# Ten buffers instead of six for the rows of x, with 4096 contiguous bytes per partition in each load and store

## The chip, the cores and the metric

The kernel runs on one NeuronCore of a Trainium2 chip. The metric is the device time of one execution in microseconds (us). The kernel before took 1952.6 us, the median of three runs (1951.16 to 1956.97 us).

## What is computed

One layer of a relational graph network with a layer norm ahead of it: 12,500 nodes of 256 floats, 212,500 edges sorted by their destination, 8 types of edges.

```
h = jnp.maximum(_layernorm(x, axis=-1), 0.0)
hx = jnp.einsum('ni,rio->rno', h, weight)            # 8 relations
agg = jax.ops.segment_sum(hx[edge_type, src], dst, num_segments=12500)
out = x + agg * 0.5**0.5 + h_bias + (h @ loop_weight) * 0.5**0.5
```

The kernel turns the sums around: for each destination and type it first adds up the rows h[src], and multiplies the eight sums of a destination by the eight weights afterwards.

## The kernel before

**Tiles and gathers.** The edges are cut into 1581 tiles of 128, two tiles to a unit. For each tile the row h[src] of each edge is fetched from DRAM into a tile msg of 128 rows by 1 KB. For most tiles that is one indirect DMA, issued by GpSimd (POOL, L936, `gather`); I number them from 0 in the order of issue. For 50 tiles far into the program the sync and scalar queues fetch single rows instead (L965). A matmul of each msg tile with a one-hot matrix (TensorE, L1031, `edge_sums`) sums rows by destination and type in PSUM, and VectorE adds the sum of each unit to a ring of accumulators (L1064, `add_sums`). Each group of 128 destinations that is complete is multiplied by the weights (L1238) and stored.

**What a gather waits for.** 33 buffers hold two msg tiles each. The first 100 gathers of the program read raw rows of x, since h isn't there yet; these take one of eight completion counters (DMASW0 to DMASW7) in turn, so that each waits until the gather eight before it has landed. Gather 100 is the first that reads h; it waits until all of h has been stored. In `goal` (L948 to L952) the order of the program lets the gathers run ahead of the sums by a count of tiles that rises by 4 for each unit; `gather` adds a wait on the last matmul of the unit before (L945, "no faster than the sums"). So gather 72, the first of its step, waits for the end of tile 25, and gather 80 for the end of tile 29. From gather 66 on a gather also needs a msg buffer that has been read.

**The normalised rows.** x is cut into 26 pieces: 24 of 512 rows (four rows of 1 KB for each of 128 partitions), one of 128 and one of 84 rows (L805 to L809). A piece goes through five steps. The sync queue (SP) loads it into a buffer xt (`load_rows`, L886). VectorE takes the statistics of each 128 rows (L828, `moments`). For each bunch of pieces ScalarE takes a root (L864) and VectorE the reciprocal (L868, in `close`). ScalarE normalises in place (L872). SP stores the piece to the DRAM tensor h32 (L895, in `rest`). ScalarE and VectorE treat the msg tiles that were gathered from x in the same way, by the same lines.

**The order around them.** The order of each engine's instructions is written out by hand (`manual_schedule`), and each engine works through its own list. Pieces 0 to 3 come first. Then the loop over the tiles t (L1441) normalises one piece in each of three steps out of four and a batch of four msg tiles in the fourth, which I call a period: 3 pieces and 4 tiles. The loop's step 28 normalises the last piece, after which `load_weights` (L1363) loads the bias, w and wl through SP, and ScalarE scales w six steps later (L1378). Since VectorE works in order, the add of unit u (L1064) stands behind the statistics of the pieces of its step: unit 9's add stands behind the statistics of piece 20, unit 11's behind those of piece 23. The matmuls of a unit need a free PSUM bank of four; the wait for it is put on the last matmul of the unit before, so the end of tile 25 waits for the add of unit 9, and the end of tile 29 for that of unit 11.

**The buffers of the pieces.** xt comes from a pool of ROWS = 6 buffers (L334). `norm_rows(i)` (L888) first issues the load of piece i + 4 into the buffer of piece i - 2, which waits until the store of piece i - 2 has ended; the store of piece i is issued later, when ScalarE has normalised it. SP works in order too: while a load waits, the stores behind it aren't issued. A DMA of SP also takes one of eight completion counters (DMAHW0 to DMAHW7) in turn, so no more than eight are on their way.

Of the kernel before, what the change touches and what calls it, by code (L numbers as in the profile page):

```python
# [9 lines left out]
F32 = mybir.dt.float32  # L10
# [13 lines left out]
P = 128  # L24
# [4 lines left out]
XG = 4  # L29
# [56 lines left out]
SHARED = 3  # L86

ROWS = 6
FIRST = 4


# [157 lines left out]
def kernel(  # L249
# [12 lines left out]
    N, D = x.shape  # L262
# [30 lines left out]
    w = const.tile([P, KC, R * D], F32, name="w")  # L293
# [34 lines left out]
    with ExitStack() as main:  # L328
# [4 lines left out]
        ep = main.enter_context(tc.tile_pool(name="ep", bufs=1))  # L333
        rowp = main.enter_context(tc.tile_pool(name="rowp", bufs=ROWS))  # L334
        idx = main.enter_context(tc.tile_pool(name="idx", bufs=2))
# [469 lines left out]
        for d in range(0, N, XG * P):  # L805
            k = min(XG, (N - d) // P)
# [3 lines left out]

        def rows_of(a, i):
            d, k, n = pieces[i]
            return a[d : d + k * n].rearrange("(k p) d -> p k d", p=n)

        bunch = []

        def moments(rows_, n, then, begun=None):

            if not bunch:
                bunch.append(small.tile([P, 2 * BATCH, 6], F32, name="stats") if begun is None else begun)  # L820
                if n < P:
                    nc.vector.memset(bunch[0], 0.0)
            stats = bunch[0]
            here = rows_ if begun is None else rows_[:-SHARED]
            for row in rows_:
                k = sum(len(r) for r, _, _ in bunch[1:])
                if begun is None or len(bunch) - 1 < len(here):
                    in_run("stats", nc.vector.bn_stats(stats[:n, k, :], row), row is here[-1])  # L828
                bunch.append(([row], n, None))
            bunch.append(([], n, then))  # L830
# [49 lines left out]
        xts = {}  # L880

        def load_rows(i):
            if i < len(pieces):
                _, k, n = pieces[i]
                xts[i] = rowp.tile([P, XG, D], F32, tag="rows", name="xt")
                nc.sync.dma_start(xts[i][:n, :k, :], rows_of(x, i))  # L886

        def norm_rows(i):  # L888
            d, k, n = pieces[i]
            xt = xts.pop(i)  # L890
            if i > 1:
                load_rows(i + ROWS - 2)

            def rest():
                nc.sync.dma_start(rows_of(h32, i), xt[:n, :k, :])  # L895

            moments([xt[:n, j, :] for j in range(k)], n, rest)

# [103 lines left out]
        def load_offsets(u0):  # L1002
            n = min(REGS, NU - u0)
            b, q = row_of(u0)
            _, vals = nc.values_load_multi_w_load_instructions(
                place[b][0:1, q : q + n], engines=[DVE], min_val=0, max_val=RING - 1,
                skip_runtime_bounds_check_because="clamped to the ring where it is computed")
            for i, v in enumerate(vals):
                offsets[u0 + i] = v
# [279 lines left out]
        with tc.manual_schedule():  # L1289

            load = prepare(0)
            load[0]()
            for i in range(ROWS):
                load_rows(i)
            make_identity(nc, ident)
            iota_i = marks.tile([P, XG * GROUP], I32, tag="mark0", name="iota_i")
# [29 lines left out]
            for i in range(2):  # L1326
                norm_rows(i)
# [19 lines left out]
            after.pop(0)()  # L1347
            for i in range(2, FIRST):
                norm_rows(i)
# [83 lines left out]
            load_offsets(0)  # L1433
            done["norm"] = FIRST
            for t in range(0, 2 * BATCH, BATCH):
# [5 lines left out]
            for t in range(NT):  # L1441
# [12 lines left out]
                if t % BATCH == BATCH - 1:  # L1454
                    if done["norm"] < len(pieces):
                        after = batch(t + 1 + BATCH)
                    elif done["scaled"] <= t + 1 + 2 * BATCH:
                        after = batch(done["scaled"], 2 * BATCH)
                        after.append(lambda t=done["scaled"]: begin_batch(t))
                elif done["norm"] < len(pieces):  # L1460
                    for i in range(1 if NT > 400 else 20):
                        if done["norm"] < len(pieces):
                            norm_rows(done["norm"])
                            done["norm"] += 1
                            if t % BATCH % 2 or NT <= 400 or done["norm"] == len(pieces):
                                after += close()
                    if NT <= 400:
                        for f in after:
                            f()
                        after = []  # L1470
                    if done["norm"] == len(pieces):
                        for f in after:
                            f()
                        after = []
                        norms_end(t)
# [91 lines left out]
```

## Time and profile before

| what | value |
|---|---|
| median of three runs | 1952.6 us |
| the profiled execution | 1951.46 us |
| its span, first to last instruction | 1949.8 us |
| TensorE busy (PE) | 1702.0 us, 87% |
| GpSimd busy (POOL) | 1455.6 us, 75% |
| VectorE busy (DVE) | 1305.0 us, 67% |
| ScalarE busy (ACT) | 157.2 us, 8% |
| mean granted TensorE clock | 0.953 |
| DMA, mean rate | 143 GB/s |
| busy share of the 16 DMA engines, 60 to 120 us | 0.98 |
| the same, 400 to 1900 us | 0.46 |

The times of the trace count from the span's start; the profiled execution took 1.7 us beyond its span. The shares are means over parts that differ: ScalarE is busy for two thirds of the first 200 us and hardly at all behind them, and the DMA engines are full in the first 120 us only, in which the pieces are loaded and stored. "Releaser" in a row is what ended the idle time ahead of an instruction; "issue" means that the profile shows none.

### The profile page before, as it was taken

What the parts mean: (1) busy time and instruction counts of PE and PEld (TensorE: products, weight loads), DVE (VectorE), ACT (ScalarE), POOL (GpSimd) and SP (SyncE); (2) the same over time, 40 slices, a digit from 0 to 9 for tenths busy, and PEclk for the clock granted to TensorE, in tenths of its full rate; (3) what the DMA queues carried; (4) which work ended last, traced back from release to release, by engine and by line L of the source; (5) the groups of instructions that cost most, each with busy time, mean ns of one, the idle gap of its engine ahead of it and who ended that gap; (6) DMA issues with size and microseconds to landing.
All of it is one profiled execution on the core that took longest, in us unless ns stands there. A gap on an engine that the chain in (4) does not pass through costs nothing.

```text
span 1949.8 us, 40539 instructions
## 1 busy us (share of the span) xinstructions
PE 1702.0 (87%) x10161; PEld 1460.0 (75%) x10161; DVE 1305.0 (67%) x3284; ACT 157.2 (8%) x333; POOL 1455.6 (75%) x1557
## 2 busy tenths in 40 slices
PE   2358999999998999889898899998889889899998
PEld 2247898998887777777777777777777777687887
DVE  7668766787765687656677665578566567665652
ACT  6778200000000000000000000000000000000000
POOL 7767777777777777777777777777777777777774
PEclk9559999999999999999999999999999999999999
DMA  9984454544444444444544444444444444444442
GB/s 291 329 281 129 125 152 123 153 133 141 122 142 131 132 143 114 138 131 121 152 132 121 141 128 124 142 121 142 131 120 140 130 125 132 121 141 126 131 121 82
DMA packets 158423, 279.41 MB, mean 143 GB/s; under 512 B 35441, under 2 KB 109191, under 8 KB 158183
## 3 DMA queue, kind: packets, MB, share of 16 engines
q0 software_dynamic: 73488, 200.77, 35.6%
q1 hardware_dynamic: 76648, 72.73, 12.1%
q10 hardware_dynamic: 8046, 3.30, 0.9%
q8 instruction: 80, 1.31, 0.3%
q14 instruction: 161, 1.31, 0.2%
HBM read 251.06 MB, written 25.60 MB: 142 GB/s over the span
## 4 chain that ended last, share of the span: by engine, by line
PE 40%; DMA 23%; POOL 20%; issue 8%; DVE 6%; ACT 3%; SPq 0%; DVEq 0%; POOLq 0%; ACTq 0%; PEldq 0%
PE po L1238 20%; DMA msg<-h,gidx 20%; POOL msg L936 20%; PE ps L1031 18%; ACT msg L872 1%; DVE acc L1064 1%; DMA h<-xt 1%; DVE stats L828 1%; DMA xt<-in_x_dram 1%; DVE acc L1106 1%; PE pt L1088 1%; ACT xt L872 1%; DMA msg<-h 1%; DVE oh L993 1%; PE pt L1137 1%
## 5 line engine op out<-in xcount | busy, mean ns | idle before, releaser
L936 POOL DMA_INDIRECT msg<-h,gidx x1431 | 1358.7, 949 | 437.4 <-issue 363.8
L1031 PEld LDWEIGHTS ps<-oh,msg 128*128 128x128 f32 x6324 | 929.1, 197 | 390.5 <-DMA msg<-h,gidx 248.4
L1031 PE MATMUL ps<-oh,msg 128*128 128x136 f32 (+1 forms) x6324 | 1010.5, 289 | 204.5 <-DMA msg<-h,gidx 120.8
L1238 PE MATMUL po<-w,acc 128*128 128x256 f32 (+1 forms) x3136 | 890.3, 389 | 7.8 <-DVE acc L1064 7.2
L1064 DVE TENSOR_TENSOR acc<-acc,ps 128x352 f32 x791 | 408.6, 517 | 391.2 <-PE ps L1031 381.9
L1238 PEld LDWEIGHTS po<-w,acc 128*128 128x128 f32 (+1 forms) x3136 | 519.4, 193 | 45.5 <-DVE acc L1064 10.4
L1106 DVE SCALAR_TENSOR_TENSOR acc<-types,pt 128x256 f32<-128x256 bf16 x688 | 248.6, 412 | 68.6 <-PE pt L1088 64.4
L993 DVE TENSOR_TENSOR oh<-fixed,cols 128x544 f32<-128x544 f32 x396 | 282.8, 714 | 0.0
L936 POOL DMA_INDIRECT msg<-in_x_dram,gidx x100 | 94.9, 949 | 39.2 <-issue 34.2
L1238 PE MATMUL po<-wl,self_t 128*128 128x256 f32 (+1 forms) x392 | 114.6, 418 | 6.8 <-DVE acc L1064 4.5
L1238 PEld LDWEIGHTS po<-wl,self_t 128*128 128x128 f32 (+1 forms) x392 | 72.9, 208 | 15.5 <-DVE acc L1064 5.6
L1226 DVE TENSOR_TENSOR xr<-xr,po 128x256 f32<-128x256 f32 (+1 forms) x98 | 40.5, 413 | 24.0 <-PE po L1238 17.3
L872 ACT ACTIVATE msg<-msg,shift,rstd 128x256 f32<-128x256 f32 x100 | 50.8, 587 | 6.3 <-DVE stats L836 4.6
L872 ACT ACTIVATE xt<-xt,shift,rstd 128x256 f32<-128x256 f32 x98 | 50.0, 587 | 13.1 <-DVE shift L869 13.1
L1253 DVE TENSOR_TENSOR xr<-xr,po 128x256 f32<-128x256 f32 (+1 forms) x98 | 41.2, 421 | 10.6 <-PE po L1238 7.3
L828 DVE BATCH_NORM_STATS2 stats<-xt 128x6 f32<-128x256 f32 x98 | 34.1, 411 | 14.9 <-DMA xt<-in_x_dram 14.6
L1088 PE MATMUL pt<-ident,hr 128*128 128x128 f32 (+1 forms) x196 | 39.0, 282 | 4.6 <-DMA hr<-h 2.7
L1093 DVE COPY self_t<-pt 128x256 f32<-128x256 f32 (+1 forms) x98 | 40.5, 414 | 3.1 <-PE pt L1088 2.9
L1160 DVE CAST types<-pt 128x512 bf16<-128x512 f32 x22 | 15.2, 691 | 40.5 <-PE pt L1156 40.5
L455 DVE TENSOR_SCALAR moves<-fixed 128x271 int32<-128x271 int32 (+1 forms) x90 | 40.5, 450 | 1.6 <-DVE acc L1064 0.5
L457 DVE COPY_PREDICATED fixed<-moves,fixed 128x311 int32<-128x311 int32 (+14 forms) x90 | 38.0, 422 | 3.1
L1088 PEld LDWEIGHTS pt<-ident,hr 128*128 128x128 f32 (+1 forms) x196 | 25.7, 152 | 7.1 <-DMA hr<-h 2.9
(166 smaller groups left out, 348.8 us busy)
## 6 DMA issues: line engine op xcount, KB each, us to landing
msg<-h ACTq DMA_DIRECT2D x3200, 1.0 KB
msg<-h SPq DMA_DIRECT2D x3200, 1.0 KB
msg<-h,gidx POOLq DMA_INDIRECT x1431, 4.7
xt<-in_x_dram SPq DMA_DIRECT2D x24, 512.0 KB
h<-xt SPq DMA_DIRECT2D x24, 512.0 KB
xr<-in_x_dram SPq DMA_DIRECT2D x23, 512.0 KB
hr<-h SPq DMA_DIRECT2D x23, 512.0 KB
out_dram<-xr SPq DMA_DIRECT2D x22, 512.0 KB
```

The costliest lines, as they stand in the source:

```text
L455: nc.vector.tensor_single_scalar(m, packed[:, :n], 1 << (bit + k), op=ALU.bitwise_and)
L828: in_run("stats", nc.vector.bn_stats(stats[:n, k, :], row), row is here[-1])
L872: nc.scalar.activation(row, row, AF.Relu, bias=shift[:n, j : j + 1], scale=rstd[:n, j : j + 1])
L936: i = nc.gpsimd.indirect_dma_start(out=msg[t], out_offset=None, in_=table[:, :], in_offset=bass.IndirectOffsetOnAxis(ap=gidx[b][:, at : at ...
L993: j = nc.vector.tensor_tensor(o[:, k : k + v, :i, :width], iota_f[:, :width].unsqueeze(1).unsqueeze(1).to_broadcast([P, v, i, width]), of. ...
L1031: j = nc.tensor.matmul(ps[:, c, first : first + width], m[:, c * P : (c + 1) * P], o[:, :width], start=(i == 0 and c == 0), stop=(end and ...
L1064: i = nc.vector.tensor_tensor(a, a, ps, op=ALU.add)
L1088: in_run("turns", nc.tensor.transpose(pst[:, c, :n], rows_[:n, c * P : (c + 1) * P], ident[:n, :n]), c == KC - 1)
L1093: nc.vector.tensor_copy(got["self", g][:, :, :n], pst[:, :, :n])
L1106: i = nc.vector.scalar_tensor_tensor(acc[:, :, r, s0 : s0 + n], of, float(r + 1), pst[:, :, :n], op0=ALU.is_equal, op1=ALU.mult)
L1238: i = nc.tensor.matmul(got["out", g][:n], lhs, rhs, start=(r == R and c == 0), stop=(r == R - 1 and c == KC - 1))
L1253: nc.vector.tensor_add(rows_[:n, k, :], rows_[:n, k, :], got["out", g][:n])
```

## The change

The number of buffers of the pieces goes from 6 to 10. The pool keeps its 6; pieces whose number modulo 10 is 6 to 9 go into four parts of the tile of the weights, w (128 x 2 x 2048 floats), which is filled with the weights only after the last piece. The load of piece i + 8 (was i + 4) is now issued behind the store of piece i, no longer ahead of the statistics of piece i; it still waits for the store of piece i - 2. Ten loads (was six) are issued at the start. And a piece's rows are dealt out differently: partition p holds the four rows 4p to 4p + 3 of the piece, which lie together in DRAM (4096 bytes), where it held the rows p, 128 + p, 256 + p and 384 + p (four stretches of 1024 bytes). Loads and stores both do so. The loads and stores of the groups at L1179 to L1184 and L1255 to L1259 stay as they were.

```diff
@@ -86,6 +86,7 @@
 SHARED = 3
 
 ROWS = 6
+STAGED = 10
 FIRST = 4
 
 
@@ -810,7 +811,7 @@
 
         def rows_of(a, i):
             d, k, n = pieces[i]
-            return a[d : d + k * n].rearrange("(k p) d -> p k d", p=n)
+            return a[d : d + k * n].rearrange("(p k) d -> p k d", p=n)
 
         bunch = []
 
@@ -882,17 +883,20 @@
         def load_rows(i):
             if i < len(pieces):
                 _, k, n = pieces[i]
-                xts[i] = rowp.tile([P, XG, D], F32, tag="rows", name="xt")
+                j = i % STAGED - ROWS
+                if j < 0:
+                    xts[i] = rowp.tile([P, XG, D], F32, tag="rows", name="xt")
+                else:
+                    xts[i] = w.rearrange("p c (a k d) -> p (c a) k d", k=XG, d=D)[:, j, :, :]
                 nc.sync.dma_start(xts[i][:n, :k, :], rows_of(x, i))
 
         def norm_rows(i):
             d, k, n = pieces[i]
             xt = xts.pop(i)
-            if i > 1:
-                load_rows(i + ROWS - 2)
-
             def rest():
                 nc.sync.dma_start(rows_of(h32, i), xt[:n, :k, :])
+                if i > 1:
+                    load_rows(i + STAGED - 2)
 
             moments([xt[:n, j, :] for j in range(k)], n, rest)
 
@@ -1290,7 +1294,7 @@
 
             load = prepare(0)
             load[0]()
-            for i in range(ROWS):
+            for i in range(STAGED):
                 load_rows(i)
             make_identity(nc, ident)
             iota_i = marks.tile([P, XG * GROUP], I32, tag="mark0", name="iota_i")
```

PE, POOL, DVE and ACT keep the order of their instructions; only names of tiles change (w in the place of xt). SP's order changes. At the start of the program SP issued, before, the last two of its six loads, then the stores of pieces 0 and 1, the loads of pieces 6 and 7 and the store of piece 2:

```order
L886 DMA xt_152<-in_x_dram 128x4x256
L886 DMA xt_154<-in_x_dram 128x4x256 [waits DMAHW0_49]
L895 DMA h32_57<-xt_144 128x4x256 [waits DMAHW3_49,DMAHW1_49,Activation_49]
L895 DMA h32_57<-xt_146 128x4x256 [waits DMAHW4_49,DMAHW2_49,Activation_49]
L886 DMA xt_291<-in_x_dram 128x4x256 [waits DMAHW1_49]
L886 DMA xt_298<-in_x_dram 128x4x256 [waits DMAHW2_49]
L895 DMA h32_57<-xt_148 128x4x256 [waits DMAHW5_49,Activation_49]
```

The same place now, from piece 4's load on (one stretch of 1024 elements for each partition, w_64 for pieces 6 to 9):

```order
L891 DMA xt_152<-in_x_dram 128x1024
L891 DMA xt_154<-in_x_dram 128x1024 [waits DMAHW0_49]
L891 DMA w_64<-in_x_dram 128x1024 [waits DMAHW1_49]
L891 DMA w_64<-in_x_dram 128x1024 [waits DMAHW2_49]
L891 DMA w_64<-in_x_dram 128x1024 [waits DMAHW3_49]
L891 DMA w_64<-in_x_dram 128x1024 [waits DMAHW4_49]
L897 DMA h32_57<-xt_144 128x1024 [waits DMAHW5_49,Activation_49]
L897 DMA h32_57<-xt_146 128x1024 [waits DMAHW6_49,Activation_49]
L897 DMA h32_57<-xt_148 128x1024 [waits DMAHW7_49,Activation_49]
L891 DMA xt_354<-in_x_dram 128x1024 [waits DMAHW5_49,DMAHW0_49]
```

Four more loads stand ahead of the first store, and the next load (piece 10) stands behind the store of piece 2. In the middle of the pieces, SP before ran from the store of piece 10 (xt_529) to the load of piece 20 (xt_842):

```order
L895 DMA h32_57<-xt_529 128x4x256 [waits DMAHW0_49,Activation_49]
L895 DMA h32_57<-xt_573 128x4x256 [waits DMAHW1_49,Activation_49]
L886 DMA xt_709<-in_x_dram 128x4x256 [waits DMAHW0_49]
L895 DMA h32_57<-xt_583 128x4x256 [waits Activation_49]
L886 DMA xt_753<-in_x_dram 128x4x256 [waits DMAHW4_49,DMAHW1_49]
L886 DMA xt_762<-in_x_dram 128x4x256 [waits DMAHW3_49]
L895 DMA h32_57<-xt_619 128x4x256 [waits DMAHW6_49,Activation_49]
L895 DMA h32_57<-xt_663 128x4x256 [waits DMAHW7_49,Activation_49]
L886 DMA xt_798<-in_x_dram 128x4x256 [waits DMAHW6_49]
L895 DMA h32_57<-xt_673 128x4x256 [waits Activation_49]
L886 DMA xt_842<-in_x_dram 128x4x256 [waits DMAHW7_49,DMAHW2_49]
```

Now, from the store of piece 10 (xt_354) to the load of piece 20 (xt_751):

```order
L897 DMA h32_57<-xt_354 128x1024 [waits Activation_49]
L891 DMA w_64<-in_x_dram 128x1024 [waits DMAHW6_49,DMAHW3_49]
L897 DMA h32_57<-xt_357 128x1024 [waits Activation_49]
L891 DMA w_64<-in_x_dram 128x1024 [waits DMAHW5_49,DMAHW0_49]
L897 DMA h32_57<-xt_528 128x1024 [waits Activation_49]
L891 DMA xt_751<-in_x_dram 128x1024 [waits DMAHW7_49,DMAHW2_49]
```

The load of piece 20 stood behind the store of piece 15 and stands behind that of piece 12 now; a store and a load alternate.

## The prediction

> **What bounds the kernel now.** I began with the page: the busiest engine is TensorE with 87% of the span, then POOL with 75%. A share doesn't say who waits for whom, so the next view is the waits, for the long middle (500 to 1900 us).
>
> ```profile
> span 1949.8 us, 40539 instructions
> PE 1702.0 (87%) x10161; PEld 1460.0 (75%) x10161; DVE 1305.0 (67%) x3284; ACT 157.2 (8%) x333; POOL 1455.6 (75%) x1557
> ```
>
> ```profile
> POOL msg L936 <- issue: 288.4, 945, 0.3
> PE ps L1031 <- DMA msg<-h,gidx: 117.9, 212, 2.6
> ```
>
> The last number of a row is the longest wait. POOL never waits longer than 0.3 us there, and TensorE waits 117.9 us for gathered rows: the gathers set the pace. The page's groups count the gathers (x1431 and x100), and the timeline of POOL shows them one by one: start, duration, and in brackets the idle time before.
>
> ```profile
> L936 POOL DMA_INDIRECT msg<-h,gidx x1431 | 1358.7, 949 | 437.4 <-issue 363.8
> ...
> L936 POOL DMA_INDIRECT msg<-in_x_dram,gidx x100 | 94.9, 949 | 39.2 <-issue 34.2
> ```
>
> ```profile
> 4.86 1.11 POOL L936 DMA_INDIRECT msg<-in_x_dram,gidx  x1 [2.23 <-DVE bound_o L1320]
> 92.76 0.94 POOL L936 DMA_INDIRECT msg<-in_x_dram,gidx  x1 [0.30 <-ACT msg L872]
> 94.01 0.95 POOL L936 DMA_INDIRECT msg<-in_x_dram,gidx  x1 [0.30 <-issue]
> ...
> 100.54 0.94 POOL L936 DMA_INDIRECT msg<-in_x_dram,gidx  x1 [5.59 <-issue]
> ...
> 112.07 0.94 POOL L936 DMA_INDIRECT msg<-in_x_dram,gidx  x1 [1.83 <-issue]
> ...
> 137.06 0.95 POOL L936 DMA_INDIRECT msg<-h,gidx  x1 [0.30 <-ACT wl L1379]
> ...
> 205.66 0.95 POOL L936 DMA_INDIRECT msg<-h,gidx  x1 [1.01 <-ACT msg L872]
> ...
> 1931.94 0.95 POOL L936 DMA_INDIRECT msg<-h,gidx  x1 [0.30 <-issue]
> ```
>
> Two gathers follow each other in 94.01 - 92.76 = 1.25 us: 0.95 busy and 0.30 idle. There are 1531 (1431 + 100), and 1530 steps of 1.25 are 1912.5 us of the 1927.1 between the first and the last. Only three gathers idle longer: gather 72 at 100.54, gather 80 at 112.07 and gather 154 at 205.66. Beyond the usual 0.30 they cost 5.29 + 1.53 + 0.71 = **7.53 us**; the rest is gathers that took a little over 0.95. So whatever happens to the pieces of x, the kernel can win 7.53 us at most, and what makes POOL wait longer is lost one for one.
>
> Why those waits? Timelines of DVE, PE and SP near 100 us:
>
> ```profile
> 96.37 1.40 DVE L828 BATCH_NORM_STATS2 stats<-xt 128x6 f32<-128x256 f32 x4 [2.89 <-DMA xt<-in_x_dram]
> 98.44 0.52 DVE L1064 TENSOR_TENSOR acc<-acc,ps 128x352 f32 x1
> 99.02 2.09 PE L1031 MATMUL ps<-oh,msg 128*128 128x104 f32 x8 [5.72 <-DVE acc L1064]
> 109.97 0.52 DVE L1064 TENSOR_TENSOR acc<-acc,ps 128x352 f32 x1
> 110.55 2.09 PE L1031 MATMUL ps<-oh,msg 128*128 128x104 f32 x8 [2.13 <-DVE acc L1064]
> ```
>
> The statistics of piece 20 wait for its load; the add of unit 9 (98.44) stands behind them; the end of tile 25 (99.02) waits for the add, and gather 72 for tile 25. Gather 80 hangs in the same way on unit 11's add at 109.97. The waits of DVE and SP between 30 and 125 us:
>
> ```profile
> DVE stats L828 <- DMA xt<-in_x_dram: 14.6, 6, 3.1
> SPq L886 <- DMA h<-xt: 54.0, 16, 6.4
> ```
>
> Late pieces hold DVE up six times, 14.6 us; SP stands 54.0 us ahead of a load until an old piece is stored, which is the missing buffer.
>
> **The change, part by part.** *Earlier loads.* The load of piece 20 was issued with 21's at 87.67, behind the store of piece 15. Now it stands behind the store of piece 12, whose normalising began at 64.35:
>
> ```profile
> 64.35 2.07 ACT L872 ACTIVATE xt<-xt,shift,rstd 128x256 f32<-128x256 f32 x4 [0.47 <-DVE shift L869]
> 87.67 6.58 SPq L886 DMA_DIRECT2D xt<-in_x_dram  x2
> ```
>
> At 64.35 + 2.07 = 66.4 it can be issued, 21 us earlier. It landed 8.7 us after its issue (96.37 - 87.67); even at double that it is there by 84. All six late loads gain about two periods in this way, so I count the 14.6 us of waits as gone.
>
> How far does unit 9's add move? ScalarE works without a pause in a period whose loads are on time. The period from 48.21 to 59.55 took 11.34 us, of which 1.89 clears an accumulator, which the periods behind 59 us don't do; so 9.5 us are left.
>
> ```profile
> 48.21 4.04 ACT L872 ACTIVATE xt<-xt,shift,rstd 128x256 f32<-128x256 f32 x8 [0.47 <-DVE shift L869]
> 57.00 1.89 ACT L1077 ACTIVATE acc<-zero 128x2048 f32<-128x2048 f32 x1
> 59.55 4.04 ACT L872 ACTIVATE xt<-xt,shift,rstd 128x256 f32<-128x256 f32 x8 [0.47 <-DVE shift L869]
> 99.35 4.04 ACT L872 ACTIVATE xt<-xt,shift,rstd 128x256 f32<-128x256 f32 x8 [0.47 <-DVE shift L869]
> ```
>
> From 59.55 to 99.35 three periods took 39.8 us; at 9.5 each they take 28.5, so everything near unit 9's add comes 11.3 us earlier. Gather 72 could then start at 100.54 - 11.3 = 89.2, but POOL reaches it at 94.01 + 1.25 = 95.26: no wait, with 6 us to spare. Gather 80: released by 112.07 - 11.3 = 100.8, reached at 95.26 + 8 x 1.25 = 105.3: no wait. -5.29 and -1.53.
>
> *Gather 154* waits for scaled msg tiles, so for ScalarE's list. That must come 7.53 us earlier for its wait to go as well. On the way stands the scaling of the weights:
>
> ```profile
> 120.18 0.46 SPq L1368 DMA_DIRECT2D w<-in_L_gnn_weight_dram  x1
> 134.79 1.91 ACT L1378 ACTIVATE w<-w 128x2048 f32<-128x2048 f32 x1 [1.15 <-DMA w<-in_L_gnn_weight_dram]
> ```
>
> Before, ScalarE got there at 133.6 and waited 1.15 us for the second half of w. Now it gets there 11.3 us earlier, 122.3. The loads of w go out when the last store has, with the last normalising, also about 11 us earlier; if the queue ahead of them is no longer than before, they land by 123.5. The parts of w used as buffers are stored long before (pieces 16 to 19). So ScalarE is some 11 us ahead behind w, 7.53 are needed: -0.71.
>
> *4096 bytes per partition.* What this does to the DMA engines the trace doesn't show. These rows are of the DMA view from 0 to 130 us (packets, MB, share of 16 engines) and the rates of 40 slices from 30 to 120 us:
>
> ```profile
> q1 hardware_dynamic: 28840, 28.24, 66.6%
> q0 software_dynamic: 4357, 11.91, 28.5%
> GB/s 308 113 258 372 309 241 223 303 393 343 149 349 394 256 345 401 310 362 401 267 347 403 282 383 407 179 314 386 303 275 378 142 329 376 360 383 326 288 298 367
> ```
>
> SP's queue used 0.666 x 130 = 86.6 us of all engines for 28.24 MB, 48 ns for a packet of 1 KB. Per byte the gathers (q0) are dearer, 28.5/11.91 against 66.6/28.24, a factor of 1.015: that bounds the loss, 1.3 us of engine time. The fastest slice, 407 GB/s, bounds the gain: 16 x 4096 bytes in 161 ns where four packets of 1 KB take 192, 16% of the 25.6 MB moved, some 12 us. I take no change, the value of SP's own row; the forecast doesn't need a gain. With none, does the DMA keep up? Ahead of piece 20 stand 21 loads and 13 stores, 17.8 MB, and 0.9 MB of indices: 18.7/28.24 x 86.6 = 57 us, and the gathers issued by 85 us, 64 of the 91 in 11.91 MB, 64/91 x 0.285 x 130 = 26 us: 83 us of engine time from about 2 us on, so piece 20 lands at 85 us. Without any delay it is needed at 96.37 - 11.3 = 85.1, and by 95.26 - (100.54 - 96.37) = 91.1 if gather 72 is not to wait. So even then the wait goes, with little to spare.
>
> *Ten loads at the start.* Gathers and pieces share the engines. From 0 to 130 us a gather lands 5.5 us after its issue, and in the quiet from 140 to 160 us 2.8 us (the row between is of the first 30 us alone):
>
> ```profile
> msg<-in_x_dram,gidx POOLq DMA_INDIRECT x95, 5.5
> ```
>
> ```profile
> msg<-in_x_dram,gidx POOLq DMA_INDIRECT x20, 5.5
> ```
>
> ```profile
> msg<-h,gidx POOLq DMA_INDIRECT x17, 2.8
> ```
>
> A gather waits for the one eight before, so POOL stalls only if landing takes over 8 x 1.25 = 10 us. Bounds: nothing, if it stays at 5.5; at double the queueing (2.8 + 5.4 = 8.2) still nothing; at four times (13.6) 0.45 us for each gather concerned. I take nothing.
>
> **The sum:** -5.29 - 1.53 - 0.71 = -7.53 us. Behind gather 154 POOL runs without a pause as before, and TensorE, which is further ahead than before, gives no new wait. The span goes to 1942.3, the profiled execution from 1951.46 to 1943.9; the median of the runs lies 1.1 us above that execution, so **1945.1 us**, -0.39%. A measurement of this kernel tells about 0.3% (5.9 us) from no change.
>
> **The rivals.** *The gathers queue behind larger packets (slower).* Place: the first 100 gathers; point: landing beyond 10 us. The wait under load, 5.5 - 2.8 = 2.7 us, is about 56 packets of 48 ns. If the engines take turns by a fixed count of packets, 56 packets of 4 KB at 192 ns are 10.8 us, landing takes 13.6 and each gather 1.70 us instead of 1.25 wherever SP's queue is that long. At the start alone, where ten loads stand in it (20 gathers by 30 us): +9 - 7.5 = 1954; over all of the pieces (82 gathers): +37 - 7.5 = 1982. For it: the DMA engines are full in this stretch (the rows under the next rival). Against it: packets of SP are outstanding only as far as SP's eight counters and its waits for stores let them. [...] Chance 0.14.
>
> *The DMA engines are the bound.* They look full, and buffers move no bytes away. The rows of two stretches, with the share and GB/s at their end:
>
> ```profile
> 60.00:90.00 30.00, 9.76 (x34) 7.99 (x34) 21.92 (x77) 22.19 (x47) 22.71 (x24) 0.50 1.01 329
> 90.00:120.00 30.00, 11.42 (x41) 9.64 (x42) 19.42 (x70) 19.59 (x42) 17.45 (x19) 0.50 0.95 325
> ```
>
> Then the loads land as late as before, or w does: if w still lands at 134.8, ScalarE stands there 12 us, and gather 154 waits the 7.5 us that the first two won. That gives 1949 to 1953. For it: shares of 1.01 and 0.95. Against it: slices of 400 GB/s beside a mean of 329 and 325, and SP's 54 us of standing. Chance 0.24.
>
> *Nothing but the buffers works*, 4096 bytes being moved in pieces of 1 KB: that is the sum above, unchanged.
>
> **How the numbers follow.** Forecast 0.62 (1943 to 1946.5), DMA-bound 0.24, queueing gathers 0.14. Faster by over 0.3% 0.62, within 0.3% 0.24, slower 0.14. The range goes from 1942 (the bound of 7.53 us from the lowest run, 1951.16, is 1943.6, less a little scatter) to 1954, the queueing at the start alone.
>
> **What would show it.** In the new profile DVE's waits for xt should be gone, gathers 72, 80 and 154 should show 0.30, and the last gather should start near 1924.4. SP should stand ahead of loads, but with nobody behind it. If the gathers' landing is over 10 us and POOL idles in the first 100 us, the queueing rival holds; if ScalarE waits for w for more than 5 us, the second. I am wrong in kind if gather 100, which needs all of h stored, waits: it had no wait at 137.06, and comes near 130.2.

## The result and the profile after

| | before | after |
|---|---|---|
| median of 6 runs each | 1952.89 us | 1943.02 us |
| lowest to highest | 1951.08 to 1956.97 | 1942.29 to 1944.04 |
| ratio, 95% interval | 1 | 0.9952 [0.9942, 0.9962] |
| profiled execution | 1951.46 us | 1942.96 us |
| its span | 1949.8 us | 1941.2 us |

The kernel is faster by 9.9 us by the medians and by 8.5 us between the two profiled executions; the forecast was 7.5. The helper functions moved: line 936 (the gather) is 940 now, 828 is 829, 872 is 873, 886 (load of a piece) is 891, 895 (store) is 897, 1378 is 1382.

First, whether POOL still stands. These are rows of its timeline after the change: the first gather, numbers 72, 80, 100 and 154, and the last.

```profile
4.72 1.11 POOL L940 DMA_INDIRECT msg<-in_x_dram,gidx  x1 [2.09 <-DVE bound_o L1324]
...
95.05 0.95 POOL L940 DMA_INDIRECT msg<-in_x_dram,gidx  x1 [0.30 <-issue]
...
105.06 0.94 POOL L940 DMA_INDIRECT msg<-in_x_dram,gidx  x1 [0.30 <-ACT rstd L865]
...
130.10 0.94 POOL L940 DMA_INDIRECT msg<-h,gidx  x1 [0.30 <-ACT unused L842]
...
197.94 0.95 POOL L940 DMA_INDIRECT msg<-h,gidx  x1 [0.30 <-issue]
...
1924.01 0.94 POOL L940 DMA_INDIRECT msg<-h,gidx  x1 [0.30 <-issue]
```

None of the 1530 gathers behind the first has more than 0.32 us of idle time ahead of it; the three long waits (5.59, 1.83 and 1.01 us) are gone. The last gather starts 1931.94 - 1924.01 = 7.93 us earlier. The first starts 0.14 earlier, the waits give 7.53, and 0.26 us is left for the small differences among 1530 steps. Behind the last gather the program ran 1949.8 - 1931.94 = 17.86 us before and 1941.2 - 1924.01 = 17.19 now. So the span is 7.93 + 0.67 = 8.6 us shorter, and all of that but 1.1 us lies in the three waits.

Next, the waits of DVE, SP and ScalarE between 30 and 125 us, after:

```profile
DVE rstd L869 <- ACT rstd L865: 14.3, 10, 4.1
DVE both L857 <- ACT stats L845: 3.0, 1, 3.0
DVE acc L1068 <- PE ps L1035: 1.1, 1, 1.1
```

```profile
SPq L897 <- ACT xt L873: 25.1, 9, 5.6
SPq L897 <- ACT w L873: 15.6, 5, 4.8
SPq L897 <- ACT rstd L865: 10.2, 7, 1.9
SPq L891 <- DMA h<-xt: 4.7, 5, 1.9
```

```profile
ACT w L1382 <- DMA w<-in_L_gnn_weight_dram: 0.8, 1, 0.8
```

DVE never waits for a piece (14.6 us before); what is left is its wait for ScalarE, 14.3 us (12.0 before). ScalarE is now the slowest of the chain that normalises: from 30 to 90 us it was busy for 54.6 of 60 us. SP's line has turned round: it stood 54.0 us at line 886 (a load that waits for an old store), and now 4.7 us at line 891, but 25.1 + 15.6 + 10.2 = 50.9 us at line 897, a store that waits for ScalarE. It still stands for more than half of the 95 us, only at another instruction. And the weights, loaded into the space that had served as buffers, come 0.8 us late.

The reciprocals of two periods show the 9.5 us period that the forecast worked out, and SP's rows show the loads of piece 20 and of w:

```profile
68.34 0.20 DVE L869 RECIPROCAL rstd<-rstd 128x8 f32<-128x8 f32 x1 [0.49 <-ACT rstd L865]
...
87.33 0.20 DVE L869 RECIPROCAL rstd<-rstd 128x8 f32<-128x8 f32 x1 [0.49 <-ACT rstd L865]
```

```profile
67.00 0.46 SPq L891 DMA_DIRECT2D xt<-in_x_dram  x1
...
106.57 0.44 SPq L1372 DMA_DIRECT2D w<-in_L_gnn_weight_dram  x1
```

```profile
120.79 1.91 ACT L1382 ACTIVATE w<-w 128x2048 f32<-128x2048 f32 x1 [0.77 <-DMA w<-in_L_gnn_weight_dram]
```

87.33 - 68.34 is two periods, 19.0 us. The second half of w is scaled at 120.79, 14.0 us earlier than before (134.79).

Last, the DMA queues from 0 to 130 us and the gathers' time from issue to landing there:

```profile
q1 hardware_dynamic: 12152, 29.93, 62.6%
q0 software_dynamic: 4751, 12.98, 29.8%
...
msg<-in_x_dram,gidx POOLq DMA_INDIRECT x100, 6.2
```

SP's queue moves 29.93 MB in 62.6% of 130 us of all engines, 2.72 us for a MB; before it was 66.6% for 28.24 MB, 3.07. That is 11% less, inside the forecast's bounds (a loss of 1.5%, a gain of 16%). A gather lands in 6.2 us at the median (5.5 before).

### The profile page after: what moved, and what is told of

Same layout as the page of the kernel before. It is cut to its first block, busy times and chain, and to the rows that moved or that the text cites. A ratio compares the mean times of both kernels' runs of the same rounds, so it can differ in the third digit from the quotient of the medians.

```text
span 1941.2 us, 40543 instructions
## 1 busy us (share of the span) xinstructions
PE 1693.9 (87%) x10161; PEld 1455.5 (75%) x10161; DVE 1305.9 (67%) x3284; ACT 156.7 (8%) x333; POOL 1455.3 (75%) x1557
## 3 DMA queue, kind: packets, MB, share of 16 engines
q1 hardware_dynamic: 58216, 72.73, 11.6%
## 4 chain that ended last, share of the span: by engine, by line
PE 41%; DMA 21%; POOL 19%; issue 8%; DVE 6%; ACT 3%; SPq 0%; DVEq 0%; POOLq 0%; ACTq 0%
PE po L1242 21%; DMA msg<-h,gidx 20%; POOL msg L940 19%; PE ps L1035 19%; ACT msg L873 1%; DVE stats L829 1%; DVE acc L1068 1%; DMA msg<-in_x_dram,gidx 1%; DVE oh L997 1%; PE pt L1092 1%; DVE moves L456 0%; PE pt L1141 0%; ACT xt L873 0%; ACT unused L842 0%; ACT w L873 0%
## 5 line engine op out<-in xcount | busy, mean ns | idle before, releaser
L873 ACT ACTIVATE xt<-xt,shift,rstd 128x256 f32<-128x256 f32 x66 | 33.7, 587 | 10.5 <-DVE shift L870 10.5
L829 DVE BATCH_NORM_STATS2 stats<-msg 128x6 f32<-128x256 f32 x79 | 27.3, 410 | 0.9 <-issue 0.9
```

The costliest lines, as they stand in the source:

```text
L873: nc.scalar.activation(row, row, AF.Relu, bias=shift[:n, j : j + 1], scale=rstd[:n, j : j + 1])
```

## The experiments

The change has three parts: the number of buffers (6 or 10), the place of the load in SP's order (ahead of the statistics of a piece, so ahead of its store, or behind that store), and the packets (1024 or 4096 bytes). My theory A said that the buffers do it. The rivals were B, that the packets do it since the DMA engines are full, and C, that the place of the load does it. Each run is compared with the kernel before on its own chip. All four kernels of the first group ran on one chip, where the kernel before took 1954.17 us (1950.19 to 1957.59, 21 runs).

### Ten buffers, load behind the store, packets of 1024 bytes

```diff
@@ of the changed kernel
-            return a[d : d + k * n].rearrange("(p k) d -> p k d", p=n)
+            return a[d : d + k * n].rearrange("(k p) d -> p k d", p=n)
```

> Ten buffers, but pieces dealt out as before (four stretches of 1024 bytes per partition). Theory A (the early loads do it): VectorE's waits for the pieces, 14.6 us before, fall under 3 us, the gathers 72, 80 and 154 idle 0.30, time 1943 to 1945.5. Rival B (the 4096-byte packets do it, because the DMA engines are the bound): the loads come late again, VectorE waits 8 us or more, time 1948 to 1953.

Measured: 1943.95 us (1942.83 to 1944.91), ratio 0.9948 [0.9934, 0.9961], the whole gain. No gather but the first idles over 0.32 us and DVE never waits for a piece. The DMA view of this kernel, 0 to 130 us:

```profile
q1 hardware_dynamic: 30584, 29.93, 70.0%
q0 software_dynamic: 4739, 12.97, 29.1%
...
msg<-in_x_dram,gidx POOLq DMA_INDIRECT x100, 5.8
```

The same 29.93 MB cost 70.0% here and 62.6% with the larger packets: 0.074 x 130 = 9.6 us of all engines saved, and no time won by it. So nothing on the way to the end waited for those engines any more. Rival B falls for the full change. The counts show what a packet is here: there are 30584 - 12152 = 18432 fewer, three for each of the 128 partitions of 24 loads and 24 stores. So a run of 1024 or of 4096 bytes counts as one packet.

So the same bytes took 10.5% less time of the engines in the larger packets: 91.0 us (0.700 x 130) with 1024 bytes, 81.4 (0.626 x 130) with 4096.

### Six buffers, load ahead of the statistics, packets of 4096 bytes

```diff
@@ of the kernel before
-            return a[d : d + k * n].rearrange("(k p) d -> p k d", p=n)
+            return a[d : d + k * n].rearrange("(p k) d -> p k d", p=n)
```

> The kernel before with six buffers and its old order of loads and stores, only the pieces dealt out with 4096 bytes per partition. Theory A: SP still stands ahead of its loads until stores have ended, each late load lands about 1 us sooner since SP's packets take 11% less time per byte, VectorE's waits fall from 14.6 to about 8 us, gather 72 still idles 1 to 3 us, time 1946 to 1951. Rival B: the whole gain, 1942 to 1944.5.

Measured: 1953.36 us (1951.75 to 1955.88), ratio 0.9998 [0.9989, 1.0007]. The larger packets alone are worth nothing; theory A's range and rival B's both had a gain in them. The gathers that idle, and the waits of DVE and SP in this kernel:

```profile
91.06 0.94 POOL L936 DMA_INDIRECT msg<-in_x_dram,gidx  x1 [1.26 <-issue]
99.78 0.94 POOL L936 DMA_INDIRECT msg<-in_x_dram,gidx  x1 [4.02 <-issue]
105.04 0.94 POOL L936 DMA_INDIRECT msg<-in_x_dram,gidx  x1 [0.56 <-issue]
112.74 0.94 POOL L936 DMA_INDIRECT msg<-in_x_dram,gidx  x1 [3.00 <-issue]
207.70 0.94 POOL L936 DMA_INDIRECT msg<-h,gidx  x1 [2.16 <-ACT msg L872]
```

```profile
DVE stats L828 <- DMA xt<-in_x_dram: 15.4, 10, 2.5
```

```profile
SPq L886 <- DMA h<-xt: 54.3, 16, 6.1
```

Beyond 0.30 each the gathers idle 0.96 + 3.72 + 0.26 + 2.70 + 1.86 = 9.5 us. SP stands 54.3 us ahead of loads, as before (54.0): a piece that takes less time of the engines (2.84 us for a MB from 0 to 130 us, 0.613 x 130 for 28.07 MB, against 3.07 before) is still asked for late.

### Six buffers, load behind the store, packets of 4096 bytes

```diff
@@ of the changed kernel
-STAGED = 10
+STAGED = 6
```

> The changed kernel with STAGED = 6: the load of piece i + 4 stands behind the store of piece i, six buffers, 4096 bytes. Theory A: a load goes out later than in the kernel before, VectorE waits longer for the pieces than 14.6 us, time 1950 to 1960. Rival B (packets): 1942 to 1945. Rival C (the order of SP does it: a store never stands behind a load that waits): 1942 to 1946.

Measured: 1949.92 us (1946.88 to 1952.54, 11 runs), ratio 0.9982 [0.9973, 0.9991]. All three expectations missed: A's time by a hair (1950 to 1960), though as a loss where this is a gain, B's by 5 us and C's by 4. With the six buffers of before, the place of the load alone brings some 0.18%, 3.5 us. The rows say how (DVE, then SP, 30 to 125 us):

```profile
DVE stats L829 <- DMA xt<-in_x_dram: 16.3, 11, 3.0
```

```profile
SPq L897 <- ACT xt L873: 58.9, 20, 6.2
```

Pieces are late as much in sum as before (16.3 us against 14.6), but spread over 11 waits; and SP never stands ahead of a load, so no store is queued behind one. Seven gathers idle for 0.37 to 1.91 us, 4.3 us beyond 0.30 in all, where before it was 7.53. The profiled execution is the fastest of the eleven, 3.0 us below their median, so the median execution probably idles longer than 4.3 us.

### Eight buffers

```diff
@@ of the changed kernel
-STAGED = 10
+STAGED = 8
```

> The changed kernel with STAGED = 8: the load of piece i + 6 stands behind the store of piece i, piece 20 is asked for behind the store of piece 14. Theory A: that is 8 to 10 us later than with ten buffers and still about 8 us ahead of need, so VectorE waits under 4 us, the waits of gathers 72 and 80 are gone, time 1942.5 to 1945. If ten buffers are needed: 1946 to 1951.

Measured: 1943.72 us (1942.84 to 1944.69), ratio 0.9947 [0.9934, 0.9961]; DVE waits 0.8 us in two waits for pieces, and no gather waits. Eight are enough; the last two of the ten buffers bring nothing that these runs show.

### Ten buffers, load ahead of the statistics, packets of 1024 bytes

This and the next run shared a chip on which the kernel before took 1957.53 us (1951.22 to 1959.82, 17 runs).

```diff
@@ of the changed kernel, beside packets of 1024 bytes
+            if i > 1:
+                load_rows(i + STAGED - 2)
             def rest():
                 nc.sync.dma_start(rows_of(h32, i), xt[:n, :k, :])
-                if i > 1:
-                    load_rows(i + STAGED - 2)
```

> Ten buffers alone: the load stands ahead of the statistics again, and packets are of 1024 bytes. The run of this kernel beside a kernel before of 2439 us told nothing, since POOL wasn't the bound there; this is the same question again. Theory A (the buffers and the age of the store waited for are what counts): with ten buffers the load of piece i+8 waits for a store that began two periods ago, so the order of SP's list hardly matters: no wait of DVE for a piece over 1 us, no gather but the first idles over 0.5 us, 1942.5 to 1945, ratio 0.995. Theory C (SP standing ahead of loads delays stores as well, and the loads must go behind): SP stands in this order too, and the time is that of six buffers with the load behind the store or worse, 1949 to 1953.

Measured: 1952.93 us (1949.76 to 1956.45, 12 runs), ratio 0.9979 [0.9971, 0.9988]. Theory A fell here: buffers alone bring 0.21%, less than half of the gain. By this ratio C held as it was put (no better than six buffers with the load behind). Where the rest is lost, in four views of this kernel (DVE, SP, POOL, ScalarE):

```profile
101.38 1.40 DVE L829 BATCH_NORM_STATS2 stats<-xt 128x6 f32<-128x256 f32 x4 [5.13 <-DMA xt<-in_x_dram]
```

```profile
SPq L891 <- DMA h<-xt: 30.5, 8, 6.4
SPq L891 <- DMA h<-w: 16.8, 4, 7.0
```

```profile
117.77 1.40 SPq L1373 DMA_DIRECT2D w<-in_L_gnn_weight_dram  x1
```

```profile
143.63 0.94 POOL L941 DMA_INDIRECT msg<-h,gidx  x1 [3.30 <-ACT unused L842]
...
151.02 0.96 POOL L941 DMA_INDIRECT msg<-h,gidx  x1 [1.06 <-issue]
```

```profile
128.51 1.91 ACT L1383 ACTIVATE w<-w 128x2048 f32<-128x2048 f32 x1 [3.48 <-DMA w<-in_L_gnn_weight_dram]
...
133.53 1.91 ACT L1383 ACTIVATE w<-w 128x2048 f32<-128x2048 f32 x1 [2.80 <-DMA w<-in_L_gnn_weight_dram]
```

SP stands 30.5 + 16.8 = 47.3 us ahead of loads although there are ten buffers (54.0 with six). The load issued at piece i waits for the store of piece i - 2 with ten buffers as with six: more buffers let SP ask for a later piece there, but the store that it waits for is no older. So theory A's "store that began two periods ago" was wrong. Ahead of the statistics at most one more store is issued between that store and the load; behind the load stand, in SP's order, the store of piece i and all that follows. So a store that lands late delays later stores, and these delay later loads; one piece holds DVE up for 5.13 us. With the load behind the store of piece i, two more stores are issued in between, each when ScalarE is done with its piece, and in the changed kernel SP stands only 4.7 us ahead of loads. At the end of the pieces SP comes to the weights at 117.77 (106.57 after the full change), ScalarE waits 3.48 + 2.80 us for them, and the wait turns up at POOL from gather 108 on. In sum the gathers idle 4.5 us beyond 0.30.

### The kernel before once more

No edit.

> The kernel before, word for word, profiled once more where POOL is the bound. If the excess of the median gain (9.9 us) over the 7.53 us of POOL's waits comes from how late pieces happen to land in each execution, this profile shows other gathers idle or for other lengths than 5.29, 1.53 and 0.71 us, and the excess of the idle gathers over 0.30 us follows the time: time less 1944 equals that excess within 1 us. If the excess is a fixed cost elsewhere, the idle gathers are the same three at 7.5 us whatever the time.

Measured: one execution of 1955.91 us. Five gathers idle in its timeline of POOL:

```profile
87.09 0.95 POOL L936 DMA_INDIRECT msg<-in_x_dram,gidx  x1 [2.09 <-PE ps L1031]
92.38 0.94 POOL L936 DMA_INDIRECT msg<-in_x_dram,gidx  x1 [0.58 <-issue]
99.89 0.94 POOL L936 DMA_INDIRECT msg<-in_x_dram,gidx  x1 [2.82 <-issue]
112.92 0.94 POOL L936 DMA_INDIRECT msg<-in_x_dram,gidx  x1 [3.32 <-issue]
207.40 0.94 POOL L936 DMA_INDIRECT msg<-h,gidx  x1 [1.57 <-ACT msg L872]
```

Beyond 0.30 they cost 1.79 + 0.28 + 2.52 + 3.02 + 1.27 = 8.9 us, at other gathers and in other lengths than the 7.53 of the first profile. So the kernel alone doesn't fix the sum of the waits; whether the execution or the chip makes this difference, two profiles can't say. The second half of the expectation missed: the time less 1944 is 11.9 us, 3 more than the waits. The last gather started at 1936.19, the first at 4.87; less the 8.9 us that leaves 1922.4 us for 1530 steps where the first profile has 1931.94 - 4.86 - 7.53 = 1919.6. This chip's steps are 2 ns longer. The profile of the kernel above, on the same chip, agrees: 1932.11 - 4.89 - 4.5 = 1922.7.

### Runs on chips where another bound held

Six runs fell on two other chips, where the kernel before itself took 2438.83 us (2426.7 to 2453.81, 23 runs) and 2409.29 us (2396.22 to 2418.66, 15 runs).

> Ten buffers alone: the load of piece i + 8 stands ahead of the statistics of piece i as in the kernel before, 1024-byte stretches as before. Theory A (enough buffers, so that a load is asked for two periods ahead): no waits of VectorE for pieces, gathers 72, 80 and 154 idle 0.30, time 1942.5 to 1945.5. Rival C (SP's order matters by itself, as the six buffers with loads behind stores suggested, which gained 4 us): 1946 to 1951.

> The changed kernel without the loads of pieces 10 to 25: these sixteen pieces aren't read, their buffers are normalised and stored again, so h is wrong from node 5120 on; 7.8 MB less go over the DMA engines. Theory A (POOL's steps of 1.25 us are the floor, nothing of the pieces is left on the path): within 1.5 us of the changed kernel, 1941.5 to 1944.5. Rival D (the full DMA engines still cost something in the first 120 us): 1935 to 1941.

> The changed kernel with SINGLE = 24: 59 tiles instead of 50 are fetched by the sync and scalar queues, 1522 gathers instead of 1531. If POOL sets the pace to the end, each gather less is worth 1.25 us: -11 us, 1930.5 to 1933.5. If TensorE or the row fetches become the bound: -5 us or less, or slower than the changed kernel.

> The kernel before once more, for its trace: its runs lie between 1950.2 and 1957.6 us, those of the kernels with eight or ten buffers between 1942.3 and 1944.9. If that scatter comes from late loads, the time over 1942.3 + 1.7 equals the idle time of gathers beyond 0.30 in this execution (7.5 us in the first trace), with other gathers or other lengths; if it comes from elsewhere, the idle time is 7.5 us again whatever the time is.

> The changed kernel with one edit taken back: the load stands ahead of the statistics, and so ahead of the store of the same piece, as before the change; ten buffers and 4096 bytes per partition stay. With 1024 bytes this order cost half the gain (ratio 0.9979): SP stood ahead of loads for 47 us with stores queued behind it, the loads of w went out late and gathers 108 to 113 idled 5 us. Theory E (the order of SP's list is worth about half, whatever the packets): the same here, ratio 0.997 to 0.9985, SP stands over 35 us ahead of loads between 30 and 125 us, and POOL idles 3 to 6 us over its 0.30. Rival F (the cheaper packets make up for the order, since with them stores land sooner): ratio 0.994 to 0.996, SP stands under 20 us, and no gather but the first idles over 0.5 us.

> The changed kernel with one number changed: every 24th tile behind the normalising (28th before) is fetched row by row by SP and ScalarE and not by a gather of POOL, so 1522 gathers in place of 1531. If POOL's gathers set the pace of this kernel, as the prediction has it, nine fewer at 1.25 us take off 11 us: 1931 to 1934 us, ratio 0.989 to 0.991 of the kernel before. If TensorE or the fetches of SP and ScalarE are as late as POOL, the time stays or rises (ratio over 0.995), and TensorE waits for fetched rows and not for gathers. The earlier run of this kernel stood beside a kernel before of 2439 us, where POOL wasn't the bound, and was 6% slower there.

| kernel | its edit | median us | ratio |
|---|---|---|---|
| ten buffers, load ahead, 1024 bytes | as above | 2440.80 | 0.9996 [0.9963, 1.0028] |
| late loads left out | pieces 10 to 25 (7.6 MB) are not loaded | 2439.04 | 0.9997 [0.9967, 1.0027] |
| more fetched tiles | `SINGLE = 24` for 28 | 2599.80 | 1.0646 [1.0604, 1.0688] |
| the kernel before | none | 2438.65 (one run) | |
| ten buffers, load ahead, 4096 bytes | as above, packets of 4096 | 2405.52 | 0.9987 [0.9969, 1.0005] |
| more fetched tiles, again | `SINGLE = 24` | 2565.82 | 1.063 [1.058, 1.068] |

POOL's waits from 500 to 1900 us in the kernel before on the first of these chips:

```profile
POOL msg L936 <- issue: 206.4, 659, 2.0
...
POOL msg L936 <- PE ps L1031: 166.6, 109, 6.6
POOL msg L936 <- remote: 162.2, 96, 2.7
```

In the first profile of this kernel the longest of these waits was 0.3 us; here gathers wait for TensorE up to 6.6 us, 166.6 us in all, all through the kernel. POOL's gathers don't set the pace there, so the three long waits of the first profile decide nothing, and SP stands only 12.5 us ahead of loads from 30 to 125 us of that profile (54.0 in the first). So the runs can't tell the theories about the buffers apart: leaving the late loads out altogether changed nothing (0.9997), and ten buffers with larger packets and the load ahead, the one corner of the three parts not measured elsewhere, stays open.

The two runs with more fetched tiles came out by their second branch, slower. The wait of TensorE for tiles whose rows are fetched one by one stands at the line that waits for their counter, L1028 before and L1032 here. This is the row of the kernel before in the first profile, over the whole run:

```profile
PE ps L1031 <- PEq L1028: 4.0, 2, 2.3
```

And this is the row of `SINGLE = 24` in its second run, from 500 to 1900 us:

```profile
PE ps L1035 <- PEq L1032: 221.6, 28, 12.3
```

On the first of these chips the same wait is 107.8 us in 25 waits over the whole run of the kernel before. So on these chips TensorE waits for the fetched rows (107.8 us against 4.0), and with nine more such tiles the second chip shows 221.6; what fewer gathers are worth where POOL sets the pace wasn't measured. Why these chips are slow stays open; the mean granted clock of the profiled executions is 0.845 to 0.882 there, against 0.953 to 0.963 on the others.

## Why the prediction was right

**The bound: right.** The forecast said that the gathers set the pace and that their waits are all there is to win. After the change POOL goes from gather 1 to 1530 without a wait over 0.32 us, and the last starts at 1924.01 (1924.4 forecast). But "7.53 us at most" holds for the one profiled execution only: the medians differ by 9.9 us.

**The waits: right in each row.** Piece 20 is loaded at 67.00 (66.4 forecast). The period is 9.5 us. The reciprocal at 87.33 stood at 98.91 before, so the work near unit 9's add comes 11.6 us earlier (11.3). Gathers 72, 80 and 154 have 0.30. Gather 100, by which I would have been wrong in kind, starts at 130.10 without a wait (130.2).

**The weights: right, with less room than it looks.** ScalarE was at the second half of w at 120.0 and waited 0.77 us; forecast were 122.3 and landing by 123.5. The load of ten buffers ahead of the statistics shows what this term costs when it fails: w 11 us later, and POOL waits 3.30 us at gather 108.

**The packets: right to take as nothing.** Engine time for a byte fell by 11%, some 9.6 us in all, and moved the end by nothing: 0.9998 alone, and 0.9948 without against 0.9952 with them.

**The rivals.** Queueing gathers fell: landing went from 5.5 to 6.2 us, and the forecast's estimate of the point from which POOL stalls was 8 x 1.25 = 10. The gathers' row for the first 140 us, after:

```profile
DMA to landing us min/median/max: 2.7/6.2/7.6
```

Even the largest is below 10. With 1024 bytes and ten buffers the median is 5.8, so four times the packet adds 0.4 us and not four times the 2.7 us of queueing. The forecast's 56 packets were worked out from these 2.7 us, not counted. That the engines take turns by a fixed count of packets was the forecast's assumption, and no run shows it: by it landing would have taken 13.6 us, and it took 6.2. That the DMA engines are the bound fell with the first experiment: the three stretches of its trace from 30 to 120 us (the last numbers of a row are the clock, the DMA share and GB/s) show the engines as busy as before, with the same packets, and it was as fast as the full change.

```profile
30.00:60.00 30.00, 14.36 (x62) 13.20 (x62) 23.45 (x84) 27.31 (x50) 22.70 (x24) 0.66 1.00 330
60.00:90.00 30.00, 12.17 (x48) 10.78 (x48) 27.71 (x98) 27.18 (x58) 22.72 (x24) 0.61 1.07 383
90.00:120.00 30.00, 13.41 (x51) 11.66 (x51) 21.52 (x79) 23.64 (x55) 22.68 (x24) 0.56 0.98 321
```

The shares are 1.00, 1.07 and 0.98. Yet from 60 to 90 us 383 GB/s were moved, where the kernel before moved 329 at a share of 1.01. So a share near 1, the rival's evidence, didn't mean that the engines could move no more: with loads asked for earlier they did.

**What the reasons had wrong.** I wrote that SP "stands 54.0 us ahead of a load until an old piece is stored, which is the missing buffer", and called the sum without the packets "nothing but the buffers works". That sum held (0.9948 with packets of 1024), but the buffers are only a part of it: the place of the load, which the reasons don't price, is another. One sign missed for the same reason, that SP should still stand ahead of loads: it stands 4.7 us ahead of loads and 50.9 us ahead of stores. The ratios of the parts:

| buffers | load | packets | ratio to before |
|---|---|---|---|
| 6 | ahead | 1024 | 1 |
| 6 | ahead | 4096 | 0.9998 |
| 6 | behind | 4096 | 0.9982 |
| 10 | ahead | 1024 | 0.9979 |
| 10 | behind | 1024 | 0.9948 |
| 10 | behind | 4096 | 0.9952 |

The buffers bring 0.21% and the place of the load 0.18%, and both together 0.5%. The two single parts were measured on different chips and with different packets (which are worth nothing where both sizes were measured), and their intervals overlap, so the runs don't say which of the two is worth more. The sum held because the row that I used, the load of piece 20 behind the store of piece 12, takes both parts together; had the change brought the buffers alone, I would have forecast 7.5 us and been off by about 3.

**The size: the forecast is 2.1 us above the measured time.** The profiled executions differ by 8.5 us, the medians by 9.9. That the median of 1943.02 lies inside the 1943 to 1946.5 to which the forecast gave 0.62 is luck: three of its six runs lie below 1943. Of the 2.1 us, 0.9 is the profiled execution (1943.9 forecast, 1942.96 measured), so the small differences beside the three waits. The rest is the 1.1 us by which the median lay above the profiled execution before and which the forecast carried over: after, the two agree within 0.1 us. So what the sum had too small is mainly the waits of the median execution, for which it took the 7.53 us of one below the median.

The runs fit that. Another execution of the kernel before idled 8.9 us at its gathers, on another chip. On the chip of the first group the profiled execution with six buffers and packets of 4096 bytes, a kernel as fast as the one before, idled 9.5 us; less these, 1953.44 leaves 1943.9, close to the profiled 1944.4 and 1944.2 of the two kernels without waits. It also fits that the kernel before scatters by 7.4 us on that chip (21 runs) and the three kernels without waits by some 2 us each (5 or 6 runs). That the whole difference of the medians comes from there is argued, not shown: none of the profiles of that group is of the kernel before itself.

## What to carry to other kernels

SP stood ahead of loads until old stores had ended for 54.0 of 95 us before, and for 47.3 with ten buffers and the load ahead. That delays twice in a list worked through in order: the load itself, and every store behind it, which frees the next buffer. So before adding buffers, see how old the store is that a load waits for, and what stands behind the waiting load. Here moving the load behind the next store was worth about as much as four buffers (0.18% and 0.21%), and only both together took all waits away. And where an engine's waits come from how transfers happen to land, read them from two or three executions: the sum of one is not that of the median (7.53 and 8.9 us in two profiles of the kernel before).

## What was not expected of the hardware

Packets of 4096 bytes saved 9.6 us of time of all DMA engines (91.0 to 81.4 us for 29.93 MB) and yet let the gathers of the other queue land only 0.4 us later (6.2 us at the median) than packets of 1024 (5.8). The profile's DMA share was no ceiling: from 60 to 90 us, with packets of 1024 bytes both times, it was 1.01 at 329 GB/s with late loads and 1.07 at 383 GB/s with early ones. And the chips differ far more than the change is worth: medians of 1952.9 to 1957.5 us in three groups of runs, 2409 and 2439 us in the two others, for the same program.
